# A four-layer graph network on one core: layer 0's start, its buffers, adj's second read, and small operations on GpSimd

## The chip, the core and the metric

One core of a Trainium2 chip runs the whole kernel. The core has TensorE (PE, matrix products into PSUM), VectorE (DVE), ScalarE (ACT, activation functions from a table that has to be loaded), GpSimd (POOL) and SyncE (SP, which issues the DMAs here). Each engine works through its own list of instructions in order and waits on semaphores where it needs another's result. The metric is the device time in microseconds (us) from start to end; lower is better.

## What is computed

128 graphs of 64 nodes with 128 features (x) and a 64 x 64 matrix adj each, about a quarter of whose entries are not zero. Four layers, each on the rectified layer norm of its input and added to it:

```python
h = jnp.maximum(_layernorm(x), 0.0); x = x + _L0_gnn_ref(h, adj, adj, ...)
h = jnp.maximum(_layernorm(x), 0.0); x = x + _L1_gnn_ref(h, adj, ...)
h = jnp.maximum(_layernorm(x), 0.0); x = x + _L2_gnn_ref(h, adj, ...)
h = jnp.maximum(_layernorm(x), 0.0); x = x + _L3_gnn_ref(h, adj, ...)
```

Layer 0 makes a filter for every edge from its weight e: 64 Gaussians of e, a product with W1, softplus, a product with W2; the filter multiplies the neighbour's features and the edge's weight squared, the results are summed over neighbours and go through two dense products with a softplus between. Layer 1 works on the hyperbolic ball:

```python
h = proj(mobius_add(proj(mobius_matvec(W, x, c), c), hyp_bias, c), c)
x_loc = clip(logmap(x_provide, x_map, c), -1000, 1000)          # for every pair of nodes
a = silu(concat([x_self, x_loc]) @ att_w1.T + att_b1)
adj_att = sigmoid(a @ att_w2.T + att_b2)
support_t = sum(adj_att * x_loc * mask, axis=2)
support_t = silu(concat([x_self, support_t]) @ mlp_w1.T + mlp_b1) @ mlp_w2.T + mlp_b2 + x_self
out = proj(expmap(support_t, h, c), c)                           # tanh, mobius_add
xt = silu(logmap0(out, c)); out = proj(expmap0(xt, c), c)        # artanh, tanh
```

Layer 2 is a product with adj normalised by row sums, layer 3 a mean over senders and a dense update.

## The kernel before

`sparse_stack` (L971) does the work; `dense_stack` (L48) is a fallback for graphs with too many edges, entered only if a flag asks for it after the first has run. The graphs go in 16 groups of 8: NP = 4 pairs, two graphs of a pair on the two halves of the 128 partitions, so that a group's features are a tile of 128 x 4 x 128. Edges are not handled as a dense 64 x 64 square: `order` sorts a graph's nodes by degree and gives every node a number of slots for its neighbours, in three classes c of slots (`BLOCKS`, L758: 512, 512 and 264 wide). `slot_k` (L1040) holds each slot's number and is compared with a node's neighbour positions to make `oh`, the 0/1 matrix from neighbours to slots.

A group passes seven stages, generator functions that `yield` at each change of engine:

- `load` (L1384): DMA of adj and x.
- `order` (L1395): degrees, sorting, the transposed adj (`adjT`), `oh`, and in `normed_x` the layer norm and layer 0's node product (`rf`, tile a2).
- `layer0` (L1512): for each class and pair `weights_of` spreads adj into slots (tile va, event va0), `squares` and `neighbours` make the neighbour factor `ra`, `duo` the Gaussians `e`, `filter_of` the filter (exp, then ln, tile ex) and its sums y0, y1, y2. It starts after event `layer0` of the group ahead, that is when all its sums are made.
- `layer1_nodes` (L1654): rest of layer 0 (softplus), layer 1's node part with its pairwise coefficients (`qd`, `mp`, `pqs`) and Sx split into three bf16 parts; event nodes.
- `layer1_edges` (L1917): for each class the scores (products with U and Sx, Silu, product with aw2b, Tanh) and their sums, event edges.
- `rest1` (L2003): the rest of layer 1, `mobius` (L1641) and `artanh_over` (L1326) on tiles of 128 x 4, one number for a node; event rest1.
- `rest2` (L2121): layers 2 and 3 and the store.

`Weave` (L875) mixes these streams. It holds an estimated duration for every instruction (`about`, L785), advances a clock for each engine, and in each step issues the waiting piece that could start first; among those within 0.05 us of each other on one engine the smaller key wins. A key is the stage's due rank (L2251) plus an offset from the table `LATE` (L808), one number for each yield of a stream. `w.ring(bufs, names)` (L1207) tells it how many buffers a tile has, so that a piece can't be issued before a buffer has been released. All this happens when the program is built: on the chip the order of each engine's list is fixed.

ScalarE's functions lie in two tables, "log" (exp, ln) and "silu" (Silu, Tanh). The loop at L2254 asks for them in turn, four loads for a group: silu until `soft_ready` of the next group, log for its softplus, silu until the group's scores (`edges_silu`) and the group ahead's `rest1_silu` are through, log until layer 0 of the group after next and the next group's node part are through. A group's stages therefore lie across some four turns of this loop, and layer 0 of one group runs beside the node part of another.

Buffers before: y0, y1, y2 and a2 one each, adj five, x two. Powers on GpSimd take their exponent from constant tiles `exps` (L1010: 0.5, -0.5, -0.25); `power` (L1282) is one GpSimd instruction on four numbers a node row.

Of the kernel before, what the change touches and what calls it, by code (L numbers as in the profile page):

```python
# [11 lines left out]
F32 = mybir.dt.float32  # L12
# [8 lines left out]
NP = 4  # L21
GROUPS = B // (2 * NP)
P = 128
# [761 lines left out]
def about(engine, op, args, kw):  # L785
# [14 lines left out]
    if engine == ACT:  # L800
# [8 lines left out]
    "attention": (0, -0.5),  # L809
    "coefs_of": (1.25, 0.75, -2.25),  # L810
    "coefs_of2": (2.75,),
    "duo": (2.5, 3.5),
    "duo2": (0, 2.5, -2),
    "filter_of": (0.75, 3, -0.25, -2.25, -2, -2.75),
    "filter_of2": (-2.75, 1.75, 2.5, 1.75, -2.5),
    "layer1_nodes": (0, -0.25, 0, 0, 0, 0, 0, 3, -3.5, 0, 0, 0, -0.5, -5.5, 0, 2.25, -1.75, 0, 0, 0,
        0, 0, 0, -2.5, 0, 0, 0, 0, 0, -1.25, 0, 0, 0, 2, 0, 0.75, 0, 0, 0, 0, 0, 0, 0, 0, 0.5),
    "neighbours": (-0.25, -3.5),
    "neighbours2": (1.25,),
    "normed_x": (0, 0, 0, 0, 0, 0, 1.5),  # L820
    "one_minus_z": (3.75,),
    "order": (-0.25, -2.75, 2.25, 0, 0, -5, 0, -3.75, 0, 1.75, -6.75, -3, 3.5, 0, 0, -2.75, -2.75,
        3.25, 1.75, 0.5),
    "rest1": (-3, 0, 0, -3, 0, 0, 0, -3.5, -1.75, 0, 0, 0, 0, 0, -1.75, 0, 0, 0, 3.75),
    "rest2": (2.25, 4.5, 0, 0, 0, 0, 0, 0, 0, 0, 0, -4, 0, -3.75, 0, 1.25, 0, 0, 0, 0, -3, 0, -2.25,
        0, -3.5, 0, 0, 1.25, 3),
    "rows": (0, -1.25),
    "rows2": (2.5,),
    "scores_of": (-1.25, -1.5, -3.5, -1.5),
    "scores_of2": (0, -3.25, 0, -3.5),  # L830
    "slots_ranks": (3.5, 0, 4.75),
    "squares": (2.25, 9.5),
    "squares2": (0, 2.75),
    "turned_from": (3.5,),
    "weights_of": (-3,),
    "weights_of2": (0, -2.5, -2.25),
# [134 lines left out]
def sparse_stack(ctx: ExitStack, tc: tile.TileContext, ins, out: bass.AP, flag):  # L971
# [39 lines left out]
    for e in (0.5, -0.5, -0.25):  # L1011
        exps[e] = const.tile([P, 2 * NP], F32, name=f"exp{len(exps)}")
        G.memset(exps[e], e)
# [26 lines left out]
    slot_k = const.tile([P, SLOTS + SLOTS % 2], BF, name="slot_k")  # L1040
    slot_r = const.tile([P, SLOTS + SLOTS % 2], BF, name="slot_r")
    rooms = [(name, k) for name in ("e2", "e4", "bR", "rt", "rs", "mask", "e1") for k in range(2)]
# [27 lines left out]
    def slots_ranks():  # L1070
        for c, blocks in enumerate(BLOCKS):
            yield on(DVE)
            at = OFFS[c]
            for k, r0, n, k0 in blocks:
                ki = edge.tile([P, 1024], I32, name="ex", tag="ex", bufs=3)
                G.iota(ki[:, 0:k * n].rearrange("q (n k) -> q n k", n=n), [[0, n], [1, k]], base=k0 - 128,
                       channel_multiplier=0)
                V.tensor_copy(slot_k[:, at:at + k * n], ki[:, 0:k * n])
                V.tensor_copy(slot_r[:, at:at + k * n].rearrange("q (n k) -> q n k", n=n),
                              bl(ident2[:, r0:r0 + n], k))  # L1080
                at += k * n
# [125 lines left out]
    w.ring(1, "sm", "sl", "two", "ys", "rf", "U", "a0", "a1", "r0", "x2")  # L1207
    w.ring(2, "va2", "ra", "th", "x", "xp", "nodes", "att", "e")
    w.ring(3, "va", "ex", "big", "oh", "x1")
    w.ring(4, "adjT")  # L1210
    w.ring(5, "adj")
# [114 lines left out]
    def artanh_over(r, s, hn):  # L1326


        E, ef, num, den, q = (ttile(f"ah{k}") for k in range(5))
# [6 lines left out]
        V.scalar_tensor_tensor(num, E, 1.0, s, ALU.add, ALU.mult)  # L1336
        V.tensor_scalar(q, E, -1.0, 1.0, ALU.mult, ALU.add)
        V.tensor_tensor(num, num, q, ALU.add)
        V.tensor_tensor(den, q, s, ALU.mult)
        V.scalar_tensor_tensor(den, den, 1.0, E, ALU.add, ALU.add)  # L1340
        V.reciprocal(den, den)
        V.tensor_tensor(num, num, den, ALU.mult)
        V.tensor_tensor(den, num, num, ALU.mult)
        V.tensor_scalar(q, den, 1.0 / 9, None, ALU.mult)
        for c in (1.0 / 7, 1.0 / 5, 1.0 / 3):
            V.scalar_tensor_tensor(q, q, c, den, ALU.add, ALU.mult)
        V.scalar_tensor_tensor(q, q, 1.0, num, ALU.add, ALU.mult)
        V.tensor_tensor(q, q, ef, ALU.add)
        V.reciprocal(den, hn)
        V.tensor_tensor(r, q, den, ALU.mult)  # L1350
# [33 lines left out]
    def load(g, st):  # L1384
        yield on(DVE, "x", "adj")
        x = st["x"] = pers.tile([P, NP, D], F32, name="x", tag="x")
        adj = st["adj"] = pers.tile([P, NP, N], F32, name="adj", tag="adj", bufs=5)
# [7 lines left out]
    def order(g, st):  # L1395
# [31 lines left out]
        def normed_x():  # L1427
# [24 lines left out]
            st["rf"] = wtile("a2")  # L1452
# [7 lines left out]
        graphs_mm(pt, adj, perm)  # L1460
        yield on(ACT)
# [21 lines left out]
        for c in range(3):  # L1483
            for at, k, r0, n in blocks_of(c):
                yield on(DVE, after=[("slots",)])
                at += OFFS[c]
                ks = slot_k[:, at:at + k * n].rearrange("q (n k) -> q n k", n=n)
                V.tensor_tensor(part(oh, at, k, n), bl(pos[:, :, r0:r0 + n], k),
                                ks.unsqueeze(1).to_broadcast([P, NP, n, k]), ALU.is_equal)
# [22 lines left out]
    def layer0(g, st):  # L1512

        yield on(DVE, "ys", after=prior(("order", g), ("layer0", g - 1), ("va1", g - 2)) + [("weights0",)])
        oh, adjT, rf, sr = st["oh"], st["adjT"], st["rf"], st["sr"]
        ys = st["ys"] = [wtile(f"y{c}") for c in range(2)]
        ys.append(wide.tile([P, 2 * NP, RC], F32, name="y2", tag="y2"))
# [123 lines left out]
    def mobius(ca, cc, xx, xy, y2):  # L1641

        den = ttile("den")
# [659 lines left out]
```

## Time and profile before

| | |
|---|---|
| three runs, median (lowest, highest) | 2124.41 us (2123.33, 2126.65) |
| the profiled execution | 2121.52 us |
| its span, first to last instruction | 2119.6 us |
| mean granted TensorE clock | 0.940 |
| instructions | 31941 |
| HBM read, written | 7.61 MB, 4.19 MB |

The profile page gives busy time per engine, the span in 40 slices, the chain of work that ended last, and groups of equal instructions. A group's line reads: code line, engine, operation, out<-in by the program's tile names (numbers left out), partitions x elements and type, count | busy us, mean ns of one | idle time of the engine just before them and what ended it. Because the kernel's engines are wrapped in a class that counts durations, every line number is that of the wrapper (L853): a group is recognised by its tiles. The two busy rows of the 40 slices show the fill, the steady middle and the drain:

```profile
PE   4869897998989898998989889898989889896773
...
DVE  5669789999999999999999999999999999897742
ACT  3767887979698887979798897969888796975531
```

DMA queues are busy 2.5% of the time.

### The profile page before, as it was taken

The numbers are of one execution on the slowest core, as the hardware profiler recorded it, in microseconds if no ns is written. First come the engines' busy times: TensorE is split into PE (matmuls) and PEld (weight loads), VectorE is DVE, ScalarE is ACT, GpSimd is POOL, SyncE is SP. The second block draws the span as 40 slices with busy tenths as digits, with TensorE's granted clock in tenths as the row PEclk, the third lists the DMA queues.
The fourth block names the chain that finished last, engine by engine and source line by source line (L and its number), as shares of the span: only waits on it lengthen the run. The fifth ranks groups of instructions, "written<-read, shape, count | busy, mean of one in ns | idle before, by whom it ended". The sixth has DMA issues, their size and how long they took to land.

```text
span 2119.6 us, 31941 instructions
## 1 busy us (share of the span) xinstructions
PE 1806.3 (85%) x11223; PEld 866.0 (41%) x11223; DVE 1847.9 (87%) x4828; ACT 1641.1 (77%) x3364; POOL 364.5 (17%) x362
## 2 busy tenths in 40 slices
PE   4869897998989898998989889898989889896773
PEld 2333343444444344444444444444434444443342
DVE  5669789999999999999999999999999999897742
ACT  3767887979698887979798897969888796975531
POOL 1011012021212203021221202121220302111121
PEclk9979999999999999999999999999999999997765
DMA  2000000000000000000000000000000000000000
GB/s 55 3 6 1 1 6 1 6 8 6 1 8 6 8 6 8 6 8 6 1 8 6 9 6 9 6 1 8 6 9 1 9 1 6 1 1 6 6 5 8
DMA packets 29531, 13.94 MB, mean 7 GB/s; under 512 B 10544, under 2 KB 29360, under 8 KB 29360
## 3 DMA queue, kind: packets, MB, share of 16 engines
q1 hardware_dynamic: 29360, 11.80, 2.1%
q8 instruction: 90, 1.47, 0.3%
q14 instruction: 81, 0.66, 0.1%
HBM read 7.61 MB, written 4.19 MB: 6 GB/s over the span
## 4 chain that ended last, share of the span: by engine, by line
PE 37%; DVE 36%; ACT 19%; issue 7%; POOL 0%; SPq 0%; DMA 0%; DVEq 0%; ACTq 0%; POOLq 0%
PE big L853 25%; PE sm L853 9%; ACT ex L853 6%; DVE va L853 5%; DVE ex L853 4%; PE sl L853 4%; ACT e L853 4%; DVE th L853 4%; DVE y L853 2%; ACT ra L853 2%; DVE ah L853 2%; DVE v L853 2%; ACT n L853 2%; DVE att L853 2%; DVE oh L853 1%
## 5 line engine op out<-in xcount | busy, mean ns | idle before, releaser
L853 PE MATMUL big<-ex,w2T 128*128 128x512 f32 (+1 forms) x768 | 320.2, 542 | 41.8 <-ACT ex L853 20.6
L853 ACT ACTIVATE ex<-big,c_L_gnn_att_b 128x1024 f32<-128x1024 f32 (+1 forms) x192 | 185.5, 974 | 105.0 <-PE big L853 103.2
L853 PE MATMUL big<-e,w1T 64*128 64x512 f32 (+1 forms) x768 | 201.5, 624 | 68.0 <-ACT e L853 47.8
L853 ACT ACTIVATE ex<-big,c_L_gnn_b 128x1024 f32<-128x1024 f32 (+1 forms) x192 | 185.7, 976 | 44.1 <-PE big L853 44.0
L853 PEld LDWEIGHTS big<-ex,w2T 128*128 128x128 f32 x768 | 131.7, 189 | 198.6 <-ACT ex L853 69.5
L853 PE MATMUL big<-va,U 64*128 64x512 f32 (+1 forms) x768 | 186.5, 563 | 29.1 <-DVE va L853 26.8
L853 PE MATMUL big<-va,a 64*128 64x512 f32 (+1 forms) x768 | 181.1, 568 | 10.7 <-DVE k_s L853 3.8
L853 PE MATMUL sl<-ex,aw2b 128*64 128x512 f32 (+1 forms) x768 | 180.7, 549 | 5.5 <-ACT th L853 4.3
L853 DVE SCALAR_TENSOR_TENSOR ex<-big,c_L_gnn_b,ra 128x1024 f32<-128x1024 f32 x128 | 163.7, 1279 | 16.0 <-PE big L853 15.6
L853 ACT ACTIVATE ex<-ex 128x1024 f32<-128x1024 f32 (+1 forms) x192 | 173.9, 925 | 0.2
L853 ACT ACTIVATE ra<-big 128x528 f32<-128x528 f32 (+1 forms) x192 | 166.3, 886 | 8.1 <-PE big L853 7.6
L853 DVE TENSOR_REDUCE y<-ex 128x128 f32<-128x1024 f32 x128 | 155.3, 1213 | 0.6
L853 ACT ACTIVATE th<-sl,hab 128x512 f32<-128x512 f32 (+1 forms) x192 | 118.1, 615 | 45.4 <-PE sl L853 45.4
L853 PE MATMUL big<-slot_r,Sx 64*128 64x512 bf16 (+1 forms) x1152 | 138.9, 346 | 0.0
L853 POOL TENSOR_TENSOR k_r<-k_r,exp 128x4 f32<-128x4 f32 x32 | 32.4, 1013 | 583.1 <-DVE k_r L853 578.7
L853 PEld LDWEIGHTS big<-e,w1T 64*128 64x128 f32 x768 | 68.9, 204 | 155.6 <-ACT e L853 55.1
L853 ACT ACTIVATE va<-va,sr 128x512 f32<-128x512 f32 (+1 forms) x192 | 123.1, 650 | 3.1 <-DVE va L853 2.9
L853 PE MATMUL big<-oh,pqs 64*64 64x512 bf16 (+1 forms) x1152 | 123.3, 348 | 0.0
L853 DVE COPY_PREDICATED va<-slot_r,big 128x1024 f32<-128x1024 uint16 (+1 forms) x96 | 106.5, 1111 | 9.7 <-PE big L853 9.7
L853 DVE SCALAR_TENSOR_TENSOR th<-th,oh 128x1024 f32<-128x1024 f32 (+1 forms) x80 | 99.2, 1240 | 13.8 <-ACT th L853 13.8
L853 ACT ACTIVATE e<-e 128x1024 f32<-128x1024 f32 (+2 forms) x144 | 106.7, 752 | 1.1
L853 PE MATMUL big<-va,ones 64*64 64x512 f32 (+1 forms) x768 | 97.4, 559 | 11.0 <-DVE va L853 11.0
(479 smaller groups left out, 3832.4 us busy)
## 6 DMA issues: line engine op xcount, KB each, us to landing
x<-in_x_dram SPq DMA_DIRECT2D x16, 256.0 KB, 2.9
out_dram<-v SPq DMA_DIRECT2D x16, 256.0 KB, 2.3
adj<-in_adj_dram SPq DMA_DIRECT2D x16, 128.0 KB, 2.3
rt<-in_L_gnn_att_w_dram SPq DMA_DIRECT2D x2, 64.0 KB, 1.9
rs<-in_L_gnn_mlp_w_dram SPq DMA_DIRECT2D x2, 64.0 KB, 2.0
wupd<-in_L_gnn_W_upd_dram SPq DMA_DIRECT2D x1, 128.0 KB, 3.6
w<-in_L_gnn_W_msg_dram SPq DMA_DIRECT2D x2, 64.0 KB, 3.3
r_L_gnn_bd<-in_L_gnn_bd_dram SPq DMA_DIRECT2D x1, 64.0 KB, 3.1
```

Source lines behind the costliest of these rows:

```text
L853: return f(*args, **kw)
```

## The change

Layer 0 of a group starts when the group ahead has made its slot weights (event va0) instead of its last sum. Its sums y0, y1, y2 and its tile a2 get two buffers. Room for these comes from three places: x has one buffer instead of two; adj has one instead of five, released when `order` has used it, and `rest2` reads adj from memory again into a tile adj2 of its own; class 1's part of `slot_k` is dropped (it is class 0's plus 8, and the comparison subtracts the 8 from the positions).

Work moves between engines. In `layer1_nodes` the bias add ahead of the softplus goes from VectorE to ScalarE, two casts of the coefficients to bf16 go to ScalarE, two subtractions on Sx (128 x 512) go to GpSimd; the mask of the pairwise series uses tile e4. In `rest1` the chains on four numbers around `mobius` and most of the artanh go from VectorE to GpSimd, with a power of -1 or -0.5 in place of reciprocals. Five steps of the artanh, with bit operations, stay on VectorE. `LATE`, the table of offsets, is replaced as a whole.

```diff
 LATE = {
...
-    "rest1": (-3, 0, 0, -3, 0, 0, 0, -3.5, -1.75, 0, 0, 0, 0, 0, -1.75, 0, 0, 0, 3.75),
...
+    "rest1": (0, 0, 0, 1.5, 0, -2.25, 0, -2, 0, 0, 0, 0, 0, 0, 0, 0, 0, 0, 0, 0, 0, 0, -3.25),
...
-    for e in (0.5, -0.5, -0.25):
+    for e in (0.5, -0.5, -0.25, -1.0):
...
-    slot_k = const.tile([P, SLOTS + SLOTS % 2], BF, name="slot_k")
+    slot_k = const.tile([P, SLOTS - OFFS[1]], BF, name="slot_k")
...
-    w.ring(1, "sm", "sl", "two", "ys", "rf", "U", "a0", "a1", "r0", "x2")
-    w.ring(2, "va2", "ra", "th", "x", "xp", "nodes", "att", "e")
+    w.ring(1, "sm", "sl", "two", "x", "adj", "adj2", "U", "a0", "a1", "r0", "x2")
+    w.ring(2, "va2", "ra", "th", "ys", "rf", "xp", "nodes", "att", "e")
...
-    w.ring(5, "adj")
...
+    def artanh_of(r, E, ef, s):
+        num, den, q, z = (ttile(f"ah{k}") for k in range(2, 6))
+        G.tensor_scalar(num, E, 1.0, None, ALU.add)
+        G.tensor_tensor(num, num, s, ALU.mult)
+        G.tensor_scalar(q, E, -1.0, 1.0, ALU.mult, ALU.add)
+        G.tensor_tensor(num, num, q, ALU.add)
+        G.tensor_tensor(den, q, s, ALU.mult)
+        G.tensor_scalar(z, E, 1.0, None, ALU.add)
+        G.tensor_tensor(den, den, z, ALU.add)
+        power(den, den, -1.0)
+        G.tensor_tensor(num, num, den, ALU.mult)
+        G.tensor_tensor(z, num, num, ALU.mult)
+        G.tensor_scalar(q, z, 1.0 / 9, 1.0 / 7, ALU.mult, ALU.add)
+        for c in (1.0 / 5, 1.0 / 3, 1.0):
+            G.tensor_tensor(q, q, z, ALU.mult)
+            G.tensor_scalar(q, q, c, None, ALU.add)
+        G.tensor_tensor(q, q, num, ALU.mult)
+        G.tensor_tensor(r, q, ef, ALU.add)
...
-        x = st["x"] = pers.tile([P, NP, D], F32, name="x", tag="x")
-        adj = st["adj"] = pers.tile([P, NP, N], F32, name="adj", tag="adj", bufs=5)
+        x = st["x"] = pers.tile([P, NP, D], F32, name="x", tag="x", bufs=1)
+        adj = st["adj"] = pers.tile([P, NP, N], F32, name="adj", tag="adj", bufs=1)
...
-            st["rf"] = wtile("a2")
+            st["rf"] = wtile("a2", 2)
...
+                if c == 1:
+                    V.scalar_tensor_tensor(part(oh, at, k, n), bl(pos[:, :, r0:r0 + n], k), -8.0, ks,
+                                           ALU.add, ALU.is_equal)
...
-        yield on(DVE, "ys", after=prior(("order", g), ("layer0", g - 1), ("va1", g - 2)) + [("weights0",)])
+        yield on(DVE, "ys", after=prior(("order", g), ("va0", g - 1), ("va1", g - 2)) + [("weights0",)])
...
-        ys = st["ys"] = [wtile(f"y{c}") for c in range(2)]
-        ys.append(wide.tile([P, 2 * NP, RC], F32, name="y2", tag="y2"))
+        ys = st["ys"] = [wtile(f"y{c}", 2) for c in range(2)]
+        ys.append(wide.tile([P, 2 * NP, RC], F32, name="y2", tag="y2", bufs=2))
...
-    def mobius(ca, cc, xx, xy, y2):
+    def mobius(E, ca, cc, xx, xy, y2):
...
-        V.tensor_scalar(flat(spn), pre, bd1, None, ALU.add)
+        act(flat(spn), pre, AF.Identity, bias=bd1)
...
+        for k in range(2):
+            yield on(ACT)
+            act(pqs[:, k], (pq, e4)[k], AF.Copy)
+            yield on(DVE)
+            V.tensor_tensor((e4, pqs[:, 2])[k], (pq, e4)[k], pqs[:, k], ALU.subtract)
...
-            yield on(DVE)
-            V.tensor_tensor(Sx if k == 0 else S3[2], Sx, S3[k], ALU.subtract)
+            yield on(POOL)
+            G.tensor_tensor(Sx if k == 0 else S3[2], Sx, S3[k], ALU.subtract)
...
         yield on(POOL)
+        G.tensor_scalar(rb, st["beta"], 1e-15, None, ALU.max)
+        power(rb, rb, -1.0)
         G.tensor_scalar(un, un2, MIN_NORM2, None, ALU.max)
+        power(ur, un, -0.5)
         power(un, un, 0.5)
...
+        G.tensor_tensor(rb, rb, un, ALU.mult)
         yield on(ACT, table="silu")
         act(k_, rb, AF.Tanh)
-        yield on(DVE)
-        V.tensor_tensor(k_, k_, ur, ALU.mult)
+        yield on(POOL, after=[("uh", g)])
+        G.tensor_tensor(k_, k_, ur, ALU.mult)
...
-        mobius(ca, cc, h2, xy, un2)
-        V.tensor_tensor(cc, cc, k_, ALU.mult)
+        mobius(G, ca, cc, h2, xy, un2)
+        G.tensor_tensor(cc, cc, k_, ALU.mult)
...
-        V.tensor_scalar(s, hn, MAXNORM, None, ALU.min)
-        artanh_over(r, s, hn)
+        G.tensor_scalar(s, hn, MAXNORM, None, ALU.min)
+        yield on(DVE)
+        artanh_parts(E, ef, s)
+        yield on(POOL)
+        artanh_of(r, E, ef, s)
+        power(hn2, hn2, -0.5)
+        G.tensor_tensor(r, r, hn2, ALU.mult)
...
-        yield on(PE, "sm", after=prior(("rest1", g), ("rest2", g - 1)) + [("weights2",)])
-        adj, adjT, x2 = (st[n] for n in ("adj", "adjT", "x2"))
+        yield on(DVE, "adj2", after=prior(("edges", g), ("rest2", g - 1)))
+        adj, adj_used = pers.tile([P, NP, N], F32, name="adj2", tag="adj2", bufs=1), w.token("adj2")
...
+        nc.sync.dma_start(out=adj, in_=adj_d[gs].rearrange("(p b) i j -> (b i) p j", b=2))
+        w.wait(5)
+        yield on(PE, "sm", after=prior(("rest1", g)) + [("weights2",)])
...
```

## The prediction

> **What bounds the kernel now.** I read the page first: busy times, then the chain of waits.
>
> ```profile
> span 2119.6 us, 31941 instructions
> ...
> PE 1806.3 (85%) x11223; PEld 866.0 (41%) x11223; DVE 1847.9 (87%) x4828; ACT 1641.1 (77%) x3364; POOL 364.5 (17%) x362
> ...
> PE 37%; DVE 36%; ACT 19%; issue 7%; POOL 0%; SPq 0%; DMA 0%; DVEq 0%; ACTq 0%; POOLq 0%
> ```
>
> No engine is alone on the chain: TensorE and VectorE hold a third each, ScalarE a fifth. The mean hides fill and drain, so I cut a steady group at ScalarE's four table loads (soft-log, silu, log, silu). Columns: stretch, length, then busy time of PE, PEld, DVE, ACT, POOL with counts, clock, DMA.
>
> ```profile
> 944.20:946.80 2.60, 2.60 (x36) 1.71 (x34) 2.55 (x5) 2.54 (x4) 1.27 (x2) 1.00 0.00 0
> 946.80:964.50 17.70, 16.18 (x146) 8.23 (x140) 17.28 (x42) 16.92 (x39) 2.67 (x3) 1.00 0.10 25
> 964.50:1026.70 62.20, 54.30 (x329) 25.86 (x329) 57.45 (x168) 58.30 (x110) 7.77 (x8) 0.97 0.02 5
> 1026.70:1065.00 38.30, 35.32 (x198) 15.86 (x199) 37.09 (x86) 24.46 (x60) 11.18 (x9) 1.00 0.01 1
> sum 242.30, PE 217.73 PEld 103.68 DVE 229.06 ACT 204.58 POOL 45.79; mean PE 27.22 PEld 12.96 DVE 28.63 ACT 25.57 POOL 5.72
> ```
>
> The sum is over two groups, so a group takes 121.15 us and holds PE 108.9, DVE 114.5, ACT 102.3, POOL 22.9. In the silu stretches VectorE is 97% busy and sets the pace; in the log stretch ScalarE (94%) does, VectorE and TensorE close behind. The next bound after VectorE is thus only 5.6 us a group away.
>
> **The change, part by part.** Durations of the moved work on VectorE, and on the engines that get it (mean ns behind the comma):
>
> ```profile
> L853 DVE TENSOR_SCALAR a<-sm,c_L_gnn_bd 128x512 f32<-128x512 f32 x16 | 11.9, 744 | 5.3 <-PE sm L853 5.3
> L853 DVE TENSOR_TENSOR n<-n,Sx 128x512 f32<-128x512 f32 x16 | 11.0, 684 | 2.6 <-ACT Sx L853 2.5
> L853 DVE CAST pqs<-e 128x256 bf16<-128x256 f32 x16 | 4.7, 294 | 0.6
> L853 DVE SCALAR_TENSOR_TENSOR ah<-ah,ah 128x4 f32<-128x4 f32 x80 | 13.0, 162 | 2.8
> L853 DVE TENSOR_TENSOR rb<-rb,un 128x4 f32<-128x4 f32 x16 | 12.7, 791 | 0.5 <-POOL un L853 0.5
> ...
> L853 POOL TENSOR_TENSOR a<-xp,o_mv 128x512 f32<-128x512 f32 x16 | 34.4, 2152 | 0.0
> L853 POOL TENSOR_TENSOR un<-un,exp 128x4 f32<-128x4 f32 x32 | 34.4, 1075 | 2.7
> L853 POOL TENSOR_TENSOR d_hn<-d_n,exp 128x4 f32<-128x4 f32 x16 | 23.2, 1448 | 1.3
> L853 POOL TENSOR_TENSOR w<-hh,cs 128x512 f32<-128x512 f32 x16 | 16.6, 1037 | 0.0
> L853 POOL TENSOR_SCALAR un<-un 128x4 f32<-128x4 f32 x32 | 9.3, 290 | 193.5 <-ACT w L853 192.1
> L853 POOL TENSOR_TENSOR k_r<-k_r,dn 128x4 f32<-128x4 f32 x16 | 5.4, 337 | 1.3
> ...
> L853 ACT ACTIVATE e<-e 128x256 f32<-128x256 f32 x48 | 20.2, 422 | 0.5
> L853 ACT ACTIVATE a<-sm 128x512 f32<-128x512 f32 x16 | 9.5, 596 | 6.5 <-PE sm L853 6.5
> ```
>
> *VectorE loses*, per group: the bias add 0.74; two casts 0.58 (the other is 284 ns); two Sx subtractions 1.37; of rest1's four-element operations 18 around mobius and 18 around artanh and the last norm, 36 x 0.162 = 5.8. Together 8.5, so 114.5 becomes 106.0. The test for layer 1's slots turns from TENSOR_TENSOR into SCALAR_TENSOR_TENSOR on the same elements; other pairs of these two forms cost the same here (th<-th,oh 1238, va<-oh,adjT 1218 ns), so 0.
>
> *ScalarE gains* the bias add, nearest the Relu from PSUM at 0.60, and two casts at 0.42: 102.3 becomes 103.7.
>
> *GpSimd gains* 6 powers at 1.04 (the usual time of un<-un,exp), 12 scalar forms at 0.23, 23 two-input forms at 0.34, and two 128x512 subtractions whose rows run from 1.04 (w<-hh,cs) to 2.15 (a<-xp,o_mv); I take 1.9 as beside a busy VectorE. 6.2 + 2.8 + 7.8 + 3.8 = 20.6: 22.9 becomes 43.5, a third of the group. Its load is no bound; its latency can be.
>
> *TensorE* keeps its 108.9 and is now the fullest engine.
>
> *The order* decides what the 8.5 is worth. In the built order of a steady group, the log stretch takes in on ScalarE one ra copy of 1024 (1.01), layer 3's four scaled copies (4 x 0.286), three 512 evacuations (0.59, 0.59, 0.58) and the two casts (0.84), and gives up two (0.58, 0.58): +3.6, so 58.3 becomes 61.9. At today's fullness (58.3 in a mean of 62.5) it lasts 66.3. TensorE does more there too: layer 3's transposes and products (0.8 + 0.7 + 3 x 1.33) and three w2T products (2.9), less two short ones and a neighbour product (1.6): +6.8, 61.5 of 66.3. That leaves the other three stretches 47.4 of TensorE's work instead of 54.1 in 58.65 (92%). VectorE, at 106, no longer fills them, so I take 93%: 51.0. Period 66.3 + 51.0 = 117.3; bounds at 96% and 90%: 115.7 and 119.0. Gain 3.85 (2.15 to 5.45) on 12 steady groups between about 418 and 1876 us: -46 (-26 to -65).
>
> *Two buffers for the sums, the earlier start of layer 0:* what they buy is in this order. Before 418 us some 2.5 groups' work lies (418 / 121, less about one for the fill); I take one group's gain, -4. Bounds: -10 (2.5 groups) and +5, if one buffer for x and adj makes the second group's order wait for its loads (2.9 and 2.3 us to landing).
>
> *Second read of adj:* 16 DMAs of 128 KB, 2.3 us each, on a queue with 2% of the engines' time. In SP's order each stands behind the x load and before the store of the group ahead, and waits for TensorE's last product with the old copy, which that store's data needs anyway. The next loads behind it are needed most of a group later. 0; without that cover 2.3 us a group.
>
> *The tail,* where nothing hides rest1 of the last group. Four-element steps with their gaps are 0.20 on VectorE and 0.31, 0.42 and 1.12 (scalar, two-input, power, each with 0.08 between) on GpSimd. Ahead of the tanh: power and product for one product, +1.3. To ca: 8 two-input, 2 scalar, 1 power, 5.1 for 11 steps' 2.2, +2.9 (cc runs under the four scalings). Artanh and s: 12 two-input, 8 scalar, 2 powers, 9.8 for 17 steps' 3.4, +6.4. One more power at the end, +1.0. Sum +12; bounds +8 (two-input at its uncontended shortest, 203 ns) and +20 (powers as slow as d_hn<-d_n,exp).
>
> *Stalls by GpSimd.* rb<-rb,un takes 791 ns where its kin take 162: in 12 of 16 groups it ends with a<-xp,o_mv, a wide GpSimd operation. Over all four-element forms this excess is 3.2 us a group for 7 wide operations, 0.45 each. Two more cost VectorE 0.9; with VectorE off the limit I count half, +5 for 12 groups (0 to +20, where every one is paid and doubled).
>
> [...]
>
> **Sum:** -46 - 4 + 12 + 5 = -33 on the span of 2119.6, 2086.6. The profiled run took 2121.5 in all and the median of the runs is 2124.4, 4.8 over the span: 2091. Its own range, not all bad ends at once: 2058 to 2118.
>
> **Rivals.**
> *A, denser:* with VectorE off the limit TensorE fills 97% of the period: 108.9 / 0.97 = 112.3, -106; with -10 and +12, 2016, median 2020. For it: no engine needs more than 109. Against: three engines within 5 us of each other, and over a whole stretch other than the 2.6 us one TensorE stays at 92% or below.
> *B, hidden:* the log stretch grows by what the silu stretches lose and the tail eats the rest: period 120.5, -8 + 12 = +4, 2128; with the head's -4, 2124.
> *C, slower: GpSimd's artanh comes too late.* From the squares to d_r: 0.23 + 1.12 + 0.31, five VectorE steps 1.0, then 7 scalar, 11 two-input, 1 power (7.9), power and product 1.5: 12.1 us. In ScalarE's built order the work between those squares and the Silu that reads d_r is three th 2.0, the bias add 0.6, two table loads 2.6, softplus 1.3, two ex 2.1, two va 1.4, one e 1.1: 11.1. It is short already, unless ScalarE idles there (today 36% of that stretch), and behind the Silu stand the scores of the layer's edges, which TensorE waits for; on GpSimd, ln_r of the next group's nodes. If each of the 18 small operations waits another 0.35 us for VectorE (d_hn<-d_n,exp loses 0.4 today), it is 6 us later; if that reaches TensorE, the period is 123.3: +26 + 12 - 4 + 5 = +39, median 2163. It decides from 2.8 us a group (33 / 12). For it: GpSimd's rows stretch beside VectorE. Against: the ScalarE slack; ACT waited for d_r only 12.9 us over the run.
>
> **Numbers.** Forecast 0.50, A 0.13, B 0.12, C 0.25. Range 2040 to 2145. From no change one can tell 0.2%, 4.2 us here: faster 0.67 (forecast, A, a third of B), same 0.07, slower 0.26.
>
> **What would show it.** Right: VectorE about 106 and GpSimd 43 a group, the four stretches near 2.6, 25, 66 and 24 us, the last store some 12 us further behind the last log table load. Wrong: ScalarE or TensorE waiting for d_r, d_ca or Sx by microseconds a group; the small GpSimd forms well over 0.4 us; a log stretch over 69 us.

## The result, and the profile after

| | before | after |
|---|---|---|
| median (lowest, highest) | 2123.87 us (2119.96, 2126.65) | 2177.53 us (2177.29, 2179.74) |
| span of the profiled execution | 2119.6 us | 2175.5 us |
| mean granted TensorE clock | 0.940 | 0.929 |
| a steady group | 121.2 us | 126.3 us |

The ratio is 1.0256, 95% interval 1.0239 to 1.0274: the change makes the kernel 2.6% slower. The prediction was 2091 us, the forecast a gain.

From the page of the changed kernel: span, engines, clock in 40 slices, and the chain of waits by line.

```profile
span 2175.5 us, 32128 instructions
...
PE 1845.0 (85%) x11223; PEld 879.1 (40%) x11223; DVE 1732.0 (80%) x4171; ACT 1656.7 (76%) x3412; POOL 678.3 (31%) x1050
...
PE 45%; ACT 24%; DVE 16%; POOL 11%; issue 3%; DMA 0%; SPq 0%; DVEq 0%; ACTq 0%; POOLq 0%
PE big L850 28%; PE sm L850 14%; ACT ex L850 9%; POOL rb L850 4%; PE sl L850 3%; DVE va L850 3%; ACT va L850 2%; DVE th L850 2%; ACT th L850 2%; POOL ur L850 2%; ACT ra L850 2%; ACT w L850 2%; ACT n L850 2%; POOL un L850 2%; DVE att L850 2%
```

VectorE fell from 87% to 80%, as it should. But GpSimd, which held nothing of the chain before, now holds 11% of it, and 4% in one tile, rb: four numbers a partition. One steady group, cut at ScalarE's table loads, with the columns of before (PE, PEld, DVE, ACT, POOL busy, then the clock):

```profile
829.47:832.07 2.60, 2.60 (x20) 1.03 (x18) 1.90 (x3) 2.54 (x3) 2.21 (x8) 1.00 0.00 0
832.07:857.81 25.74, 23.35 (x196) 11.41 (x192) 21.68 (x49) 24.20 (x59) 13.97 (x22) 1.00 0.00 1
857.81:925.16 67.35, 60.08 (x361) 29.86 (x361) 59.01 (x163) 61.95 (x118) 10.50 (x10) 0.97 0.05 13
925.16:955.77 30.61, 26.25 (x129) 10.60 (x129) 24.35 (x43) 14.55 (x35) 16.36 (x26) 0.89 0.00 1
```

The loads of three engines are the forecast's: VectorE 106.9 a group, ScalarE 103.2, GpSimd 43.0. TensorE is busy for 112.3 where 108.9 was forecast. The lengths are 2.6, 25.7, 67.4 and 30.6 us where 2.6, 25, 66 and 24 were forecast. The miss is mostly in the last silu stretch, and there the clock is lowest, 0.89. Two groups of instructions, and then that stretch as a timeline (start, length, engine, what; in brackets the idle time before, and what ended it):

```profile
L850 POOL TENSOR_TENSOR rb<-rb,un 128x4 f32<-128x4 f32 x16 | 64.6, 4035 | 1.3
...
L850 POOL TENSOR_TENSOR ah<-ah,ah 128x4 f32<-128x4 f32 x112 | 34.6, 309 | 9.2
```

```profile
1566.27 2.27 DVE L850 TENSOR_TENSOR oh<-pos,slot_k 128x2048 bf16<-128x2048 bf16 x1
...
1566.79 5.30 POOL L850 TENSOR_TENSOR rb<-rb,un 128x4 f32<-128x4 f32 x1
...
1568.46 1.21 DVE L850 TENSOR_TENSOR va<-oh,qd 128x1024 f32<-128x1024 bf16 x1
...
1569.60 2.27 DVE L850 SCALAR_TENSOR_TENSOR oh<-pos,slot_k 128x2048 bf16<-128x2048 bf16 x1
1571.80 0.23 DVE L850 TENSOR_TENSOR oh<-pos,slot_k 128x80 bf16<-128x80 bf16 x1
1572.12 0.20 ACT L850 ACTIVATE k__14678<-rb 128x4 f32<-128x4 f32 x1 [4.87 <-POOL rb L850]
...
1573.96 1.97 PE L850 MATMUL sl<-ex,aw2b 128*64 128x512 f32 x4 [3.65 <-ACT th L850]
```

The product rb*un begins while VectorE is in the first comparison oh, and ends when VectorE's fourth two-input instruction in a row ends: 5.30 us for an instruction that takes 0.20 in the drain. It does so in 12 of 16 groups. ScalarE's Tanh waits 4.87 us for it; the scores stand behind the Tanh in ScalarE's list, and TensorE waits 3.65 us for them. Then the same products, 1.08 us elsewhere, take 1.97. The same place in another group in windows of 2 us (clock: third number from the end):

```profile
938.00:940.00 2.00, 0.86 (x8) 0.20 (x4) 2.00 (x2) 0.00 (x0) 2.00 (x1) 1.00 0.00 0
940.00:942.00 2.00, 0.00 (x0) 0.00 (x0) 0.58 (x2) 1.33 (x3) 1.44 (x6) 0.82 0.00 0
942.00:944.00 2.00, 1.49 (x4) 0.29 (x4) 0.00 (x0) 1.46 (x2) 1.69 (x6) 0.50 0.00 0
944.00:946.00 2.00, 2.00 (x6) 0.66 (x6) 0.75 (x1) 1.47 (x5) 1.05 (x5) 0.50 0.00 0
946.00:948.00 2.00, 2.00 (x10) 0.60 (x8) 2.00 (x4) 0.51 (x3) 0.00 (x0) 0.50 0.00 0
```

After the gap TensorE works at half clock for 6.83 us. So the trace offers two causes, a hold and a clock. I began with the first alone.

### The profile page after: what moved, and what is told of

Its sections match the earlier page's. It is cut to its first block, busy times and chain, and to the rows that moved or that the text cites. A ratio compares the mean times of both kernels' runs of the same rounds, so it can differ in the third digit from the quotient of the medians.

```text
span 2175.5 us, 32128 instructions
## 1 busy us (share of the span) xinstructions
PE 1845.0 (85%) x11223; PEld 879.1 (40%) x11223; DVE 1732.0 (80%) x4171; ACT 1656.7 (76%) x3412; POOL 678.3 (31%) x1050
## 4 chain that ended last, share of the span: by engine, by line
PE 45%; ACT 24%; DVE 16%; POOL 11%; issue 3%; DMA 0%; SPq 0%; DVEq 0%; ACTq 0%; POOLq 0%
PE big L850 28%; PE sm L850 14%; ACT ex L850 9%; POOL rb L850 4%; PE sl L850 3%; DVE va L850 3%; ACT va L850 2%; DVE th L850 2%; ACT th L850 2%; POOL ur L850 2%; ACT ra L850 2%; ACT w L850 2%; ACT n L850 2%; POOL un L850 2%; DVE att L850 2%
## 5 line engine op out<-in xcount | busy, mean ns | idle before, releaser
L850 PE MATMUL big<-ex,w2T 128*128 128x512 f32 (+1 forms) x768 | 334.0, 559 | 18.0 <-ACT ex L850 13.6
L850 PE MATMUL sl<-ex,aw2b 128*64 128x512 f32 (+1 forms) x768 | 192.4, 581 | 69.9 <-ACT th L850 58.9
L850 PE MATMUL big<-e,w1T 64*128 64x512 f32 (+1 forms) x768 | 188.6, 586 | 31.2 <-ACT e L850 26.9
L850 PE MATMUL big<-va,U 64*128 64x512 f32 (+1 forms) x768 | 195.0, 586 | 19.4 <-DVE va L850 17.1
L850 PEld LDWEIGHTS big<-ex,w2T 128*128 128x128 f32 x768 | 136.6, 196 | 162.1 <-issue 89.7
L850 DVE SCALAR_TENSOR_TENSOR ex<-big,c_L_gnn_b,ra 128x1024 f32<-128x1024 f32 x128 | 163.6, 1279 | 35.8 <-PE big L850 18.1
L850 DVE SCALAR_TENSOR_TENSOR th<-th,oh 128x1024 f32<-128x1024 f32 (+1 forms) x80 | 108.6, 1357 | 101.1 <-ACT th L850 101.1
L850 ACT ACTIVATE ra<-big 128x1024 f32<-128x1024 f32 (+1 forms) x192 | 167.6, 883 | 5.8 <-PE big L850 5.3
L850 POOL TENSOR_TENSOR k_r<-k_r,exp 128x4 f32<-128x4 f32 x32 | 35.1, 1098 | 342.9 <-DVE k_r L850 332.3
L850 POOL TENSOR_TENSOR n<-n,Sx 128x512 f32<-128x512 f32 x16 | 18.5, 1158 | 337.6 <-ACT Sx L850 337.6
L850 DVE TENSOR_TENSOR va<-oh,adjT 128x1024 f32<-128x1024 bf16 (+6 forms) x160 | 118.9, 787 | 1.7 <-PE big L850 1.1
L850 PE MATMUL big<-oh,pqs 64*64 64x512 bf16 (+1 forms) x1152 | 117.7, 347 | 0.8 <-ACT e L850 0.8
```

The costliest lines, as they stand in the source:

```text
L850: return f(*args, **kw)
```

## The experiments

A period below is the time between the same table load of successive groups. The unit beside it, 3.413 us, is the width of the grid on which every change of the clock lies, in every run (41 changes in the trace of before, 65 in that of after, none over 2 ns off it). "Loss" is half of the half-clock time in one group: what the half clock takes at most.

| kernel | median us | ratio to before (95%) | period us | in 3.413 us | loss us |
|---|---|---|---|---|---|
| before | 2123.9 | | 121.2 | 35.5 (two are 71.0) | 2.6 |
| after | 2177.5 | 1.0256 (1.0239-1.0274) | 126.3 | 37.00 | 5.1 |
| e1 product on VectorE, too early | 2217.0 | 1.0448 (1.0431-1.0466) | 127.7-129.6 | four are 151.0 | 9.4 |
| e2 chain on VectorE, too early | 2275.5 | 1.0725 (1.0707-1.0743) | 133.1 | 39.00 | 12 |
| e3 Sx on VectorE | 2183.5 | 1.0283 (1.0266-1.0300) | 126.3 | 37.00 | 5.1 |
| e4 layer 0's start back | 2172.9 | 1.0245 (1.0224-1.0266) | 126.3 | 37.00 | 5.1 |
| e5 product left to ScalarE | 2171.3 | 1.0226 (1.0209-1.0244) | 126.3 | 37.00 | 6.8 |
| e6 run of VectorE broken | 2176.8 | 1.0253 (1.0236-1.0271) | 126.3 | 37.00 | 6.8 |
| e9 TensorE busy in the gap | 2183.4 | 1.0290 (1.0273-1.0307) | 126.3 | 37.00 | 6.8 |
| e8 chain on VectorE, new plan | 2302.1 | 1.0836 (1.0818-1.0854) | 121-148 | not fixed | 5.1-13.7 |
| f1 after, clock up | 2141.3 | 1.0100 (1.0079-1.0121) | 122.8 | 35.99 | 1.7 |
| f2 before, clock up | 2100.9 | 0.9909 (0.9892-0.9927) | 119.9 | 35.14 | 0 |
| e10 chain on VectorE, in place | 2138.5 | 1.0082 (1.0059-1.0106) | 122.9 | 36.00 | 3.4 |
| f4 after, clock up further | 2136.2 | 1.0080 (1.0051-1.0108) | 122.1, 123.8 | 35.8, 36.3 | 0.9 |
| f5 e10, clock up | 2100.9 | 0.9898 (0.9880-0.9915) | 120.2 | 35.2 | 0 |
| g1 f2, chain on GpSimd | 2128.2 | 1.0026 (1.0016-1.0036) | 122.0 | 35.7 | 0 |
| b1 f5, last artanh on VectorE | 2096.1 | 0.9888 (0.9870-0.9906) | 120.2 | 35.2 | 0 |
| b2 b1, clock up in the tail | 2094.8 | 0.9878 (0.9861-0.9894) | 120.2 | 35.2 | 0 |
| b3 f2, clock up in the tail | 2096.3 | 0.9880 (0.9863-0.9896) | 119.9 | 35.1 | 0 |

### One part undone at a time: e1 to e4

In e1 and e2 `Q` issues on VectorE but books its time on GpSimd, so that the rest of the order stays.

```diff
+    Q = Timed(nc.vector, POOL, w)
...
-        G.tensor_tensor(rb, rb, un, ALU.mult)
+        Q.tensor_tensor(rb, rb, un, ALU.mult)
```

> Only the product rb*un of rest1 (four elements a partition) is issued on VectorE; the written-out order is the changed kernel's, because its cost is still booked on GpSimd. Theory T1 (held product): the last silu stretch is 30.6 us instead of the forecast 24 because GpSimd's rb<-rb,un lasts 5.3 us in 12 groups behind VectorE's run of two-input operations, and ScalarE's Tanh and all behind it wait. Then the product takes 0.2 to 0.9 us, the stretch falls to 25 to 27 us, the period from 126.3 to 121.3 to 122.5, and the time by 12 x 4 to 12 x 5.1: 2177.5 becomes 2116 to 2130. Rival T2 (the new order itself: an earlier layer 0 makes the log stretch 67.4 us) and rival T3 (Sx subtractions on GpSimd) expect 2168 to 2180: the Tanh comes earlier, but what follows it waits for something else.

Measured: 2217.0, slower by 40 us; no theory had that. The product takes 0.16 us, but from VectorE's waits in e1 (total us, times, longest):

```profile
DVE rb L850 <- POOL un L850: 57.1, 16, 3.8
```

The product is issued with the step that begins with GpSimd's powers, so it stood some 4 us too early in VectorE's list, and everything behind it waited 3.6 us a group. TensorE's longest gap became 4.5 us. This run tests its own placing, not the theory. e2 has the same fault.

```diff
-        G.tensor_tensor(k_, k_, ur, ALU.mult)
+        Q.tensor_tensor(k_, k_, ur, ALU.mult)
...
-        power(den, den, -1.0)
+        recip(Q, den, den)
```

> The whole four-element chain of rest1 from rb*un on (the products around mobius, the artanh, with reciprocals in place of the powers of -1 and the last -0.5) is issued on VectorE, in the changed kernel's written-out order. T1: the held product was nearly all of it, so this is near e1: VectorE gets about 5.5 us a group back (106.9 to 112.5), and gains what the other small operations were held for (about 4 us a group in the trace, some of it on the way to ScalarE): 2095 to 2135, the tail 5 to 9 us shorter. Rival T1b (every held small operation counts in full, not the product alone): below e1 by another 40 us or more. T2 and T3: 2165 to 2180.

Measured: 2275.5, above every range. Here, too, VectorE waits for GpSimd's un before the product, 57.3 us in 16 groups. Its period is 133.1 us in every group, 39.00 units.

```diff
-            G.tensor_tensor(Sx if k == 0 else S3[2], Sx, S3[k], ALU.subtract)
+            Q.tensor_tensor(Sx if k == 0 else S3[2], Sx, S3[k], ALU.subtract)
```

> Only the two subtractions on Sx (128 x 512) go back to VectorE, in the changed kernel's order. T1: they lie in the log stretch, away from the held product, and VectorE has room there (59.0 of 67.4): 2172 to 2182. T3 (wide GpSimd operations stall VectorE and delay Sx by 2.4 us a group): the log stretch falls by 1 to 2.5 us, 2148 to 2166.

Measured: 2183.5, 1.5 us above T1's range, with the steady period unchanged. T3 falls.

```diff
-        yield on(DVE, "ys", after=prior(("order", g), ("va0", g - 1), ("va1", g - 2)) + [("weights0",)])
+        yield on(DVE, "ys", after=prior(("order", g), ("layer0", g - 1), ("va1", g - 2)) + [("weights0",)])
```

> Layer 0 starts again only after event layer0 of the group ahead; all else as changed, so the order is planned anew with the changed kernel's offsets. T2 (the early start makes the order worse: more in the log stretch): the log stretch returns to 62 to 64 us and the time falls by 20 us or more, to 2125 to 2157. T1: the start is not what costs; the time stays within 15 us unless the new plan happens to move the product away from the run of two-input operations, which the trace shows: 2163 to 2195.

Measured: 2172.9, stretches 2.6, 25.8, 67.5 and 30.5: layer 0's earlier start as such moves nothing with these offsets. T2 falls in this form.

### The hold and the clock, one at a time: e5, e6, e9, e8

```diff
-        G.tensor_tensor(rb, rb, un, ALU.mult)
+        w.ran(POOL, 0.19)
         yield on(ACT, table="silu")
-        act(k_, rb, AF.Tanh)
+        w.ran(ACT, 0.08)
+        for p in range(NP):
+            nc.scalar.activation(k_[:, p:p + 1], un[:, p:p + 1], AF.Tanh, scale=rb[:, p:p + 1])
```

`w.ran` books time on an engine without issuing anything, so that the rest of the order stays.

> The product rb*un is left out: four Tanh activations of one element a partition take rb as their scale and un as their input. VectorE's and TensorE's lists stay the changed kernel's word for word, so VectorE can't come to wait for GpSimd's powers as it did with the product in its own list (first experiment: 57 us, TensorE idle 4.5 us instead of 3.64 a group, then half clock). T1 (the held product, with the half clock that follows TensorE's 3.64 us gap, is the loss in the last silu stretch): the Tanh comes some 4 us earlier, the gap falls below 2.5 us, the half clock there goes; the stretch falls from 30.6 to 24 to 27 us: 2100 to 2145. Rival T1c (the hold moves on: the next GpSimd step, k*ur, is held by the same run of VectorE, d_ca comes no earlier, and ScalarE waits there instead): gap and half clock stay, 2155 to 2180. T2 (order): 2168 to 2180.

Measured: 2171.3. T1c: GpSimd's next step takes the hold over, and ScalarE waits for d_ca instead. Two lines of e5's timeline:

```profile
1567.65 4.02 POOL L850 TENSOR_TENSOR k__14698<-k__14698,ur 128x4 f32<-128x4 f32 x1 [1.35 <-ACT k__14698 L2086]
...
1576.30 1.28 ACT L850 ACTIVATE w<-hh,d_ca 128x128 f32<-128x128 f32 x4 [4.61 <-POOL d_ca L850]
```

But the last silu stretch is 29.0 us instead of 30.6, and the log stretch 69.1 instead of 67.4: what the one gains the other loses, and the period is the same to 0.1 us.

```diff
                     V.tensor_tensor(part(oh, at, k, n), bl(pos[:, :, r0:r0 + n], k), ks, ALU.is_equal)
+                if k * n * NP > 1024:
+                    nc.vector.tensor_reduce(ttile("gap"), bones.rearrange("q (p k) -> q p k", p=NP), AX.X,
+                                            ALU.add)
```

> As the changed kernel, with one more small VectorE instruction after each of the two large comparisons oh (a reduction of 128 elements to 4, some 0.2 us, of a kind beside which the trace shows no GpSimd operation held); all else and every order the same. T1d (GpSimd gets no turn between two-input VectorE operations that follow each other without a gap, but does beside another kind): rb<-rb,un ends with the first oh, 0.3 to 2.3 us instead of 5.3, and the time falls to 2095 to 2150. Rival T1e (GpSimd gets its turn only when VectorE's queue is empty, or the length of the hold has another cause): it still takes 5.3 to 5.6 us, 2176 to 2184.

Measured: 2176.8, the mechanism as T1d said, the time as T1e said. With the reduction behind the first oh, rb*un ends with that oh (1.80 us instead of 5.30 in the median); k*ur is then held for 3.21 us behind the next two operations. The period is again 126.3.

```diff
             used()
+            if c == 0 and p == 2 and w.rings["sm"][1][-1] is not None:
+                idle = bank()
+                for _ in range(10):
+                    nc.tensor.matmul(flat(idle), lhsT=bones_b, rhs=slot_r[:, 0:512], start=True, stop=True)
```

> As the changed kernel, with ten bf16 products of 128 x 512 into the idle sum bank (nobody reads them), in TensorE's list where it waits 3.64 us in the last silu stretch; 10 x 0.22 to 0.25 us leave a gap of about 1.3 us. The hold stays as it is. T4 (the half clock after the gap is part of the loss: 6.83 us at 0.50 in each group): the clock of that stretch goes from 0.89 to 1.00, TensorE's 6 us of half speed give 2 to 3 us a group back, 2140 to 2160. Rival (after the gap TensorE waits for others anyway, its clock costs nothing): 2172 to 2182.

Measured: 2183.4, just above the rival's range, though the clock of the stretch did rise to 1.00 and its length fell by 2.6 us. Log stretch and last silu stretch of e9:

```profile
979.30:1049.30 70.00, 64.08 (x361) 30.99 (x361) 59.05 (x163) 62.17 (x117) 10.50 (x10) 0.90 0.05 12
1049.30:1077.30 28.00, 25.90 (x139) 10.94 (x139) 23.84 (x43) 14.46 (x35) 16.98 (x26) 1.00 0.00 1
```

The half clock has moved into the log stretch (0.97 there in the changed kernel, 0.90 here). Three different cures, and the same period to 0.03 us: that is what led to the grid.

In e8 rest1 is the old one, with its old offsets, in a plan made anew. 

> rest1 as in the kernel before (its chains on VectorE, its offsets), planned anew so that VectorE's list has them where the planner wants them; buffers, layer 0's start, adj's second read and layer 1's moves as changed. T1: without the held chain the rest of the change is worth something: VectorE 112.5 a group, TensorE and the log stretch as changed, 2090 to 2135. T2 (the early start and the new order are the loss): 2150 to 2200.

Measured: 2302.1 with periods from 121 to 148 us. The offsets of the rest belong to another plan; this run says how much the order can cost, and nothing on T1 or T2.

### The half clock away: f1, f2, f4

```diff
+    def keep_busy(n, tag, room=None):
+
+        if w.rings[tag][1] and w.rings[tag][1][-1] is None:
+            return
+        idle = bank() if tag == "sm" else slot_bank()
+        idle = flat(idle) if tag == "sm" else idle
+        for _ in range(n):
+            nc.tensor.matmul(idle, lhsT=bones_b, rhs=slot_r[:, 0:512], start=True, stop=True)
...
+            if w.fresh:
+                w.fresh = False
+                keep_busy(6, "sl")
             pre = big()
```

`w.fresh` is set by the table load that opens the log stretch. 

> The changed kernel with bf16 products of 128 x 512 that nobody reads (some 0.23 us each) in front of the four places where TensorE waits longest in a group: 10 in the last silu stretch (gap 3.64 us), 6 after the log table load (gap 1.79), 4 and 5 in the log stretch (gaps 1.27 and 1.53). No other instruction and no engine's order is changed. In the runs so far the changed kernel and four edits of it all have a group period of 126.3 us, which is 37.00 windows of 3.413 us, and every change of the clock lies on a grid of that width: what one stretch gains another loses. Theory T5 (clock lock): TensorE runs a window or two at half clock after each window in which it was less than about half busy, and this loss adjusts itself until the period is a whole number of windows, so that only taking the half clock away frees the time: period 118 to 123 us, clock above 0.97 in the steady part, 2085 to 2140. Rival T6 (the half clock is a sign of waiting, not its cause): the clock rises and the period stays within 1 us of 126.3, 2165 to 2185.

Measured: 2141.3, 1.3 us above T5's range, period 122.8. T6 falls: the half clock is a cause, since products that nobody reads only add work and the kernel got faster. One half-clock window (one unit of the grid) a group is left, and the period still is 36 units.

f2 is the same with 9 such products at the log table load and 4 before a product of the silu stretch. 

> The kernel before with such products at its two longest waits of TensorE in a group: 9 after the log table load (gap 3.05 us, after which the clock is halved for 3.4 or 6.8 us in turn; two periods are 71.0 windows) and 4 in the silu stretch (gap 1.23). T5: the period falls from 121.2 to 118 to 120 us, 2085 to 2110. T6: 2115 to 2128. If f1 comes out below this run by about 4 us a group, the predicted gain was there and the clock took it.

```profile
939.60:942.20 2.60, 2.60 (x36) 1.73 (x34) 2.55 (x6) 2.54 (x4) 1.27 (x2) 1.00 0.00 0
942.20:959.90 17.70, 16.82 (x148) 8.61 (x145) 17.28 (x42) 16.94 (x39) 2.73 (x3) 1.00 0.09 24
959.90:1021.10 61.20, 54.14 (x336) 25.66 (x333) 56.73 (x167) 58.09 (x109) 7.73 (x8) 1.00 0.02 5
1021.10:1059.50 38.40, 36.27 (x203) 16.24 (x204) 37.16 (x87) 24.52 (x62) 11.19 (x9) 1.00 0.00 1
```

Measured: 2100.9, no half clock in the steady groups, period 119.9 (35.14: not on the grid). T5 holds here as well. But f1 is above this run by 2.9 us a group, not below.

```diff
+        keep_busy(3, "sl")
         pt = pairs_mm(sT, lambda p: w2g)
```

> The changed kernel with the filling products of f1 and three more in front of the product with w2g, where f1's trace shows the one half-clock window a group that is left. The hold on GpSimd stays. T5: without that window the period loses 1 to 2 us more, 120.8 to 122 us, 2115 to 2132, and is no longer a whole number of windows. If it stays at 36.0 windows (122.8 us, 2138 to 2145), another window takes its place. The kernel before with its clock up has 119.9; what is left between the two is then the hold and the order.

Measured: 2136.2, between the two ranges. A group without half clock takes 122.1 us; every second one has a half-clock window in another place and takes 123.8.

### The hold away, and both: e10, f5, g1

```diff
         power(un, un, 0.5)
-        G.tensor_tensor(rb, rb, un, ALU.mult)
+        yield on(POOL)
+        Q.tensor_tensor(rb, rb, un, ALU.mult)
```

and the steps from k*ur to d_cc on Q. 

> The changed kernel with rest1's product rb*un and the 14 steps from k*ur to d_cc on VectorE, this time placed in its list behind the first large oh comparison, where the powers they need are done (the first and second experiment put the product some 4 us too early); every other instruction of every engine stands as in the changed kernel. No filling products. The hold is gone for both steps. T5 (the clock locks the period): the last silu stretch is 4 us or more shorter, and the period settles on whole windows again, 36.0 (122.9 us) at most one window less than 37.0: 2130 to 2180. Rival T1 (the hold is the loss and the clock only follows it): the period falls freely to 117 to 121 us, 2070 to 2120.

Log stretch and last silu stretch of e10:

```profile
965.80:1034.30 68.50, 61.54 (x361) 30.40 (x361) 59.28 (x163) 62.14 (x118) 10.51 (x10) 0.95 0.05 12
1034.30:1058.70 24.40, 22.82 (x125) 9.63 (x123) 23.61 (x51) 14.38 (x34) 6.48 (x9) 1.00 0.00 1
```

Measured: 2138.5, period 36.00 units: T5. The stretches are 4.2, 25.7, 68.5 and 24.4: the last silu stretch is the forecast's 24 once the hold is gone. Of its 6.2 us the first stretch (4.2 for 2.6) and the log stretch (68.5 for 67.4, clock 0.95) take 2.7 back.

f5 is e10 with 19 filling products a group, placed as its text says. 

> The kernel of the run before last (product and steps to d_cc on VectorE behind the first oh comparison) with filling bf16 products at its longest waits of TensorE: 3 before the product with w2g, 6 after the log table load, 4 and 6 in the log stretch; orders otherwise the changed kernel's. Both the hold and the half clock are away. T7 (the forecast's relief was there, hidden by the two): the half clock in the steady groups is gone, the stretches near 4, 26, 65 and 24 us, period 117.5 to 120.5, 2070 to 2110, below the kernel before with its clock up (2101). Rival T2 (the change's order is itself no better than the old one): 121 to 123 us, 2115 to 2140, even with the clock up.

```profile
920.40:924.60 4.20, 3.93 (x28) 1.69 (x30) 4.06 (x12) 2.57 (x4) 2.66 (x8) 1.00 0.00 0
924.60:950.30 25.70, 23.48 (x195) 11.36 (x191) 21.62 (x50) 24.17 (x59) 14.59 (x24) 1.00 0.01 2
950.30:1016.10 65.80, 62.12 (x378) 30.44 (x377) 59.05 (x163) 61.78 (x118) 10.56 (x10) 1.00 0.05 13
1016.10:1040.60 24.50, 22.83 (x125) 9.63 (x123) 23.71 (x51) 14.46 (x35) 6.48 (x9) 1.00 0.00 1
```

Measured: 2100.9, the same as f2, period 120.2 against 119.9. Taking away the hold and the half clock gives 77 us, and what is left of the change is worth nothing that can be measured: T7's period and time, but not its gain on f2, and in that T2 is right. With the hold f5 also takes the chain's longer steps off GpSimd (in f4 ScalarE waits up to 1.4 us for d_ca besides 4.9 for rb); the runs don't separate the two.

g1 moves the product and the steps to d_cc to GpSimd in f2, with `H = Timed(nc.gpsimd, DVE, w)` to keep the old order. 

> The kernel before with its clock up (13 filling products a group, period 119.9, 2101 us), and of the whole change only rest1's product rb*un and the steps from k*ur to d_cc moved to GpSimd (one power for a reciprocal), in the old order. T1 (small GpSimd steps beside VectorE's two-input operations are held): in the old order, too, they stand beside the oh comparisons; several of them last over 1 us, ScalarE's Tanh and the scaling by d_ca come 3 to 8 us later, period 121.5 to 127, 2120 to 2185. Rival (chain has slack, VectorE is relieved of 2.4 us a group): period 118 to 120, 2080 to 2103.

Measured: 2128.2, 2.0 us a group above f2. It is T1's time, but the mechanism is one step removed: rb*un itself takes 0.20 us in the median here. It stands in GpSimd's list behind two wide operations, a<-xp,o_mv and xp<-xp,r_L_gnn_bd, that lie beside the two large oh comparisons: they last 2.52 and 3.19 us in the median, and 1.04 and 1.26 at their shortest. In the group at 927 us ScalarE's Tanh waits 3.1 us for the product and the scaling by d_ca another 2.2. So the chain's move costs in the old order, too, through GpSimd's queue.

### The tail: b1, b2, b3

```diff
+        if g < GROUPS - 1:
+            artanh_of(r, E, ef, s, G)
...
+            artanh_of(r, E, ef, s, Q)
```

> f5 with the artanh chain of the last group alone on VectorE. The prediction's tail step said 9.8 us on GpSimd against 3.4 on VectorE for 22 and 17 steps, 6.4 us on the path that sets the end. If that term is right: 2100.9 becomes 2093 to 2097. If something hides it: 2099 to 2102.

Measured: 2096.1. From the last log table load to the end 146.2 us instead of 153.1 in f5: 6.9 us in these two executions, 6.4 expected; the medians differ by 4.9, and b1's four runs go from 2091.4 to 2099.8.

b2 and b3 fill TensorE's waits in the last group's rest1 and rest2. 

> b1 with filling products also in front of TensorE's steps of the last group's rest1 and rest2 where the plan leaves it idle for over 0.8 us (at most 12 each, 75 in all): in the tail the clock is at half for about 100 of 150 us. T5 (the half clock costs on the path): TensorE holds some 40 us of the tail's path; half of it saved at best, 2075 to 2092. Rival (a filling product that is still running delays the next real one as much as the clock gives): 2092 to 2102.

> f2 (the kernel before with its clock up, 2101 us) with the same filling in the tail of the last group. T5: 2080 to 2094. Rival: 2094 to 2104.

Measured: 2094.8 and 2096.3, both in the rival's range. Against b1 that is nothing (the tail 147.0 us for 146.2): the half-clock stretches of 34 and 28 us at the end shrank to 24, 7 and 5 us, and the end came no earlier. Against f2 it is 4.6 us. Both kernels with their clock up, the changed one also with its chain back on VectorE, take the same time, 1.2% less than the kernel before; with b1 they are the fastest of this study.

## Why the prediction was wrong

The step that failed is "VectorE, at 106, no longer fills them, so I take 93%: 51.0", the length of the three stretches outside the log stretch, with its bounds of 90 and 96%. They take 58.9. The period was to be 117.3 and is 126.3. Besides that share the sum had nothing for a hold on GpSimd's small steps in the steady groups and nothing for the clock. The runs divide the 9.0 us:

- *Work and fullness, 2.9.* With neither hold nor half clock (f5) the three stretches are 54.4, 3.4 over the forecast, and the log stretch is 65.8, 0.5 under it. TensorE has 49.6 us of work in the three (50.2 less three filling products of 0.23), where the forecast counted 47.4, and 58.4 in the log stretch (62.1 less 16), where it counted 61.5. At the forecast's own 93% the 49.6 would take 53.3, so 2.3 of the 3.4 are work that it had put into the log stretch. The other 1.1 is fullness: 91%, no more than the 92% before. Taking work off VectorE did not make these stretches denser.
- *The hold, 1.9.* From f4's free group (122.1) to f5 (120.2), with the chain's longer steps on GpSimd in it.
- *The half clock, 4.2.* From 126.3 to 122.1. In the kernel before it costs 1.3 (121.2 against 119.9 in f2).

The last two depend on the order in which they are taken away: e10, which takes the hold alone, shortens the period by 3.4 us, and its loss by half clock falls by 1.7 at the same time. In all e10 gains 39 us on the changed kernel, f4 41, both 77.

By its own steps: The loads of VectorE, ScalarE and GpSimd were right within 1 us. TensorE's 108.9 was carried over from a trace with half clock in it (f2, without, has 109.8 less 13 filling products, 106.9) and came out as 112.3, with more half clock. The log stretch was right to 1.1 us, with less of TensorE's work in it than forecast. "What they buy is in this order" was right for layer 0's earlier start (e4), and the second read of adj costs nothing visible (DMA 0% of the chain). The head was put at -4; the log load that opens the steady part comes at 416.5 us instead of 418.5. The tail was put at +12 and is +5.8 from the last log load to the end; of its terms only the artanh was tested, and its size fits (6.9 for 6.4); the other 5.6 did not show in the sum. "Stalls by GpSimd" looked at the wrong side: it priced what VectorE loses to wide GpSimd operations (0.45 us each), and the loss was what small GpSimd operations wait for VectorE. The shape of it stood in the text as rival C ("GpSimd's rows stretch beside VectorE"), whose 2163 was the nearest number, but at the wrong place (artanh and d_r instead of the Tanh before them) and at 0.35 us an operation: one operation lost 5.1. That 2163 came so near is luck: it had nothing of the clock.

The clock stood in none of the cases. It could be read in the profile of before: its log stretch had 0.97, which is one half-clock window after the 3.05 us that TensorE waits at the table load. A forecast of a denser kernel has to ask where TensorE will still wait; here those waits came back as lost clock.

What stays open: why f5 stays at 120.2, with TensorE busy for 108.0 us of its own work (112.4 less 19 filling products of 0.23), ScalarE 103.0 and VectorE 108.4; and whether offsets found anew for f5's order would use the room.

## What to carry to other kernels

Before small operations go to GpSimd, look at what VectorE runs at that moment: beside a run of operations with two SBUF inputs even four numbers waited until the run ended (5.30 us), and the price was paid by the engines whose queues waited behind them (ScalarE 4.87 us, TensorE 3.65). When several different repairs leave the time the same, read the clock by windows: this loop, whose TensorE was idle for about 2 or more of the 3.41 us of some windows, was held at a whole number of windows (37.00 in the changed kernel and five edits of it), and only keeping TensorE at work freed it (13 filling products of 0.23 us a group in the waits gave the kernel before 0.9%). Taking VectorE below the limit (114.5 us a group before, 108.4 in f5) did not make TensorE's work denser here: it filled 91% of the three stretches in f5, 92% before.

## What the runs showed of the hardware

*The hold.* Of the four-element GpSimd operations in the changed kernel, 95 began while VectorE was in an operation of 512 elements or more with two SBUF inputs: 94 were stretched by over 0.2 us, 1.29 us in the mean. Beside COPY_PREDICATED none of 144 was, beside operations with one input from PSUM none of 26. The hold of rb*un lasted over instructions that follow each other directly: 5.30 us over four of them, 1.80 when a reduction stands behind the first (e6).

*The clock's grid.* In all 19 kernels every change of the clock lies on a grid of 3.413 us, the 106 changes of before and after within 2 ns of it. Of the windows of this grid at full clock (300 to 1850 us), 284 of 285 with TensorE under 45% busy were followed by half clock, and none of 7016 with 75% or more; from 50 to 70% busy it was 50 of 552 (in before and after alone 35 of 35, none of 715, and 4 of 69). At half clock the clock came back after 333 of 335 windows that were 90% busy or more, and after none of 160 under 80% (in before and after 38 of 38, and none of 23). A window that was more than half idle was enough: in before and after half clock followed all 39 of those at full clock. In the changed kernel's log stretch waits of 1.52, 0.52 and 0.52 us, one soon after the other between 882.9 and 886.6 us, are followed by 3.41 us of half clock.

*The lock.* The changed kernel and e3, e4, e5, e6 and e9 all have a period of 37.00 windows, e10 and f1 36.0, e2 39.00, two groups of the kernel before 71.0, four of e1 151.0; f2, f5 and g1, without half clock, lie off the grid (35.14, 35.2 and 35.7). e8, with half clock, has no fixed period. That the waits slide along the grid until the half clock makes up for what was gained is argued from this; the runs show the lock, and that f2, f5 and g1, without half clock, don't have it.
